# Residual stream kept in token rows, turned by VectorE and DRAM instead of TensorE, with three sequences of the first layer ahead

## The chip, the cores and the metric

The kernel runs on one core of one Trainium2 chip. Its engines work side by side, each through its own list of instructions in order: PE (matrix products), DVE (vector), ACT (scalar functions), POOL (a general engine) and SP, which here issues all transfers. The metric is the device time of one execution in microseconds (us). All arithmetic is fp32.

## The reference

The input x is (8 sequences, 512 tokens, 256 features). With xn = layernorm(x), the output is x + s * silu(g).

- s is one causal attention over xn with rotary positions, one head of 256.
- g is a transformer of two layers over xn, each with eight heads of 64 and a window of 128 tokens:

```
h = shift_token(x)                 # second half of the features comes from the token before
q, k, v = split(h @ wqkv)          # 256 -> 3 * 512
q, k = l2norm, scale, rotary with xpos
x = x + local_attention(q, k, v) @ wo
h = shift_token(x)
h = (h - mean) / sqrt(var + eps) * lg + lb       # over the shifted 256 features
a, g = split(h @ w1 + b1)                        # 256 -> 2 * 682
x = x + (a * gelu(g)) @ w2 + b2
```

Because the shift stands ahead of the layernorm, the mean and variance of a token mix the first 128 features of this token with the last 128 of the token before.

## The kernel before

A sequence has four tiles of 128 tokens. A *slot* is one layer of one sequence, (b, l); there are 16. They run in the order (0,0), (1,0), (0,1), (2,0), (1,1), ... (7,0), (6,1), (7,1). For each slot: `project` makes q, k and v of each tile (matmuls "qkv"), DVE, ACT and POOL rotate and norm them (tiles r, side, sq, ss, rn), `turn_out` transposes blocks of 32x32 on DVE into rt and sends them to DRAM (away) in an order from which `turns_in` loads qT and kT already transposed. `all_scores` multiplies them ("sps"), masks and exponentiates, `p_out` and `p_in` turn the probabilities in the same way through p_away, `all_sums` multiplies with v ("ops"), `all_outs` multiplies with wo ("wop") and adds to the residual stream, and `feed_forward` does the rest ("ff" is w1, "w2p" is w2). Within layer 0, `start` also does the plain layernorm of x and the causal attention (matmuls "qk", "v0p", "sc", "av"); it parks its result s in DRAM. `finish` loads s and x again, applies silu, multiplies, adds and stores.

The residual stream of a sequence lies in xT with features as partitions: two halves of 128 features, each with 512 tokens as columns; the shift by one token is a matter of which columns a matmul reads. So whatever needs tokens as partitions is transposed on PE against an identity: x itself on arrival (xTp), the stream ahead of the second layernorm (hps), the result ahead of silu (yps). PE also turns the causal probabilities (pT0p). Ahead of ff, normed rows xh are turned back through hn and DRAM (`blocks_back`); the last slot works in two halves of 256 tokens and uses PE for this (hT).

What runs when on PE is written out: the string ORDER names, by a letter per job, which job takes its next step. A planner (class Order) goes through it, keeps a time line for every engine with estimated durations (the numbers in `order.on`, `LAND`, `send`), and places the instructions of DVE, ACT, POOL and SP in the order in which these estimates come due; `keep` fixes that order. On the chip each engine follows its list strictly and waits where an input is missing.

Loads of layer 0's weights come after a block of 32 small transfers that clear parts of eight DRAM areas (`clear_p_aways`), and layer 1's come one by one behind the first steps (`late_loads`).

Of the kernel before, what the change touches and what calls it, by code (L numbers as in the profile page):

```python
# [15 lines left out]
P = 128  # L16
# [22 lines left out]
HALF2 = T + 1  # L39
# [5 lines left out]
    "H2JHFHGH4FHFEF2JHFENEH3FHEHFH2EGF3HF2D2H2ECFHCJGJ2ED2CENF2ECEJ2GFDBJFJCDECJFEJGECBEFC2J"  # L45
    "DFDEFJ2FA2BJIEFJFGFC3J2FJED2CEJBJN2GN2A2IECI2NCF2NFIBNFEN2D2CINFE2N2RICICI4ND2NICIFE2BN"
    "F2NRCDCDAFAENF2EBCENCFKNK2CR2ERDFRFBFRDACEAEF2EKCRDCRFRFKR2EFDEBEFKECRF2RDCDCFKCKEK2BD2"
    "FC2A2E2RFEF2EBCDC2DEKR2CKLFBCF2EFRA2DLDCFLKF2RFCE2BEC2LKEDLELDFBF2CERCFECFAD2FAFL2CE2F"
    "L2D2E2BCECLF3BOLCFEDCDAOAC2OELFBCFOEFCF2E2OLBM2D2FCMFOAEAMOF2OMEFCDCDCOEFOEFOPEBVCDFCFO"
    "EFPFBDEFCRFAFDEDVFE2AVC2OFPVBPVCVCVCOD2BEFCVECEPF3VDFDCAPAVFPVFEBC2FPCFEFEFPD2BEVPFCEPE"  # L50
    "F3PFD2VEFSAEC2AEVS2CVFVBEDSECPCPDQBCSFEVFACSFDCDVQF2ASCBQF2QVCEFESQVEFCZVSD2BETFSFCF2E2"
    "ZSFESD2T2CZCACEAZEZSETZ2STFBECDCDETFZFZBDCDFEFCTECFAFAWBCE2CTECZTFDFDBTFTFECATZD2ZCWAF2"
    "WFEWETEWFZCZCEFTD2BEFC2EZUFUZCFZBCEWUFW2CD2ZAUWACBUF3ZEWCXF2CEWFWXBdD2EZF2CFEFEWdZDC2DC"
    "XdFEA2E2dWBCX2EFXCd3BD2CEFEFdCd2F2E2XFdFD2EACXFAXCBEDEDCdFXF2EXCXFd2BCECDEDdF3ACaCEFXAa"
    "dFaD2BC2FXEBaFC2aFEFdCFEAEdAYFdYEdD2CBYFCFYabF2Ea2YCaFaD2CBEChFEdEa2AFbAFh2EbCD2bFEahEb"
    "CahF2EbFBED2hChEFChbEBD2bF2EFCAEC2bFABECDECDFbeCFEbF2BF2bFeCAD2eCEFACE2bFe2hCBCDFDFChb"
    "E3BC2F2DEeCDAF2eFEACeEeBDECDhFcF2E2FCe2hfeBCE2CD2CfFfF2A2CFecBfCEhfEFCeBD2fECcFEF2EhA2E"
    "F2fD2iFC2fEfFcfCD2BC2F2CEfFBfEFCECAEAiFiFiBD2C2FEiFEfFfDEDEC2ghi4Ei3BD2iCicAhF2CFEAFCBC"
    "EFj2CFjEF2BhA2FjDhE2jh2F2DECFgFhCDEjDgCFgFjEjECjEBC2gjED2EjBjFC2A2DCl2DlCj2klBCk2lkl2C"
    "l3BlA2nkn2l2n2m3on7ono2"  # L60
# [19 lines left out]
class Order:  # L80
# [12 lines left out]
        "quarters": {"full": 0.22, "rows": 0.2, "columns": 0.165, "eighths": 0.165},  # L93
        "eighths": {"full": 0.22, "rows": 0.2, "columns": 0.165, "quarters": 0.165},
# [150 lines left out]
def gated_attention_kernel(  # L245
# [27 lines left out]
    counts = {"x": 1, "xT": 4, "r": 7, "rt": 1, "v0": 1, "oT": 1, "hn": 1, "hid": 1, "tok": 2}  # L273
# [66 lines left out]
    def send(dst, src, after, us):  # L340

        sync.dma_start(dst, src)
        return order.on("SP", 0.42, after) + us
# [28 lines left out]
    for l in range(DEPTH):  # L372
        sc = buffer("tok", [P, 4, DH], f"sc{l}")
# [3 lines left out]
        vec_sb = weights.tile([P, 3 * KC + 2 * HC], F32, tag=f"vec{l}", name=f"vec{l}")  # L377
# [8 lines left out]
    def loads_of(l):  # L386
# [8 lines left out]
        def queries():  # L395
            load(f"wqkv{l}", wqkv_sb, wqkv[l].rearrange("(k p) n -> p k n", p=P))
# [10 lines left out]
        def second():  # L407
            load(
                f"w2{l}", w2_sb[:, 0 : HC - 1, :], w2[l, 0:whole].rearrange("(k p) n -> p k n", p=P)
            )  # L410

            for n in range(KC):
                on, cols = n * DH, slice(n * P, (n + 1) * P)
                load(f"w2{l}", w2_sb[on : on + TAIL, HC - 1, cols], w2[l, whole:HID, cols])

        return [attention, queries, output], [lambda: first(0), lambda: first(1), second]
# [14 lines left out]

    before, behind_x = loads_of(0)
# [4 lines left out]
    scale_tables(0)  # L437

# [3 lines left out]
    def layernorm(dst, src, n, name, at=0.0, groups=False):  # L442


        kind = name[0]
        few = 2 if kind == "x" else 4
        stats = small.tile([P, n, 6], F32, tag=f"stats{kind}", name=f"stats_{name}", bufs=few)
        mv = small.tile([P, n, 2], F32, tag=f"mv{kind}", name=f"mv_{name}", bufs=few)
        for i in range(n):
            vector.bn_stats(stats[:, i], src[:, i])  # L450
            end = order.on("DVE", 0.41, at, opens=f"stats{kind}")
        for i in range(n):
            vector.bn_aggr(mv[:, i], stats[:, i])
            at = order.on("DVE", 0.16, end, opens=f"mv{kind}")
        rstd = small.tile([P, n], F32, tag=f"rstd{kind}", name=f"rstd_{name}", bufs=few)
        gpsimd.tensor_scalar(rstd[:, 0:n], mv[:, 0:n, 1], EPS, None, ALU.add)
        at = order.on("POOL", 0.23, at, opens=f"rstd{kind}")
        inv_sqrt(rstd[:, 0:n], rstd[:, 0:n], n)
        at = order.on("POOL", 0.4 + 0.16 * n, at)
        for i in range(n):  # L460
            to, some = dst[:, i], src[:, i]
            if groups:
                to = to.rearrange("p (g c b) -> p c g b", g=4, c=KC)
                some = some.rearrange("p (c g b) -> p c g b", g=4, c=KC)
            vector.tensor_scalar(
                to, some, mv[:, i, 0:1], rstd[:, i : i + 1], ALU.subtract, ALU.mult
            )
            end = order.on("DVE", 0.54 if kind == "h" else 0.41, at, opens="tok" if kind == "h" else "")
        return end

    slots = [(0, 0)]
    for b in range(1, BATCH):
        slots += [(b, 0), (b - 1, 1)]
    slots.append((BATCH - 1, 1))
    stream, gated = {}, {}
# [9 lines left out]
    def start(b):  # L487
        yield {"free": {"x": 1, "xT": 1} if b else {"xT": 1}}
# [3 lines left out]
        xt = x_tiles.pop(b)  # L492
# [3 lines left out]
        xT = buffer("xT", [P, 2 * T + 1], f"xT_{b}")  # L496
        nc.gpsimd.memset(xT[:, T : T + 1], 0.0)
        yield {"at": at, "free": {"bank": 2}}
        for c in range(KC):
            ps = bank(f"xTp_{b}_{c}").rearrange("p (a b) -> p a b", a=NT)  # L500
            for t in range(NT):
                transpose(ps[:, t, :], xt[:, t, c * P : (c + 1) * P])
            at = evacuate(xT[:, c * HALF2 : c * HALF2 + T], ps.rearrange("p a b -> p (a b)"))
            free(f"xTp_{b}_{c}", at)
        free(f"x_{b}")
        stream[b] = xT
        done("started", b, at=at)

# [6 lines left out]
        for n in range(2):  # L515
            even, odd = rot[n]
            for e in range(2):
# [6 lines left out]
                for k in range(KC):  # L524
# [3 lines left out]
                        xT[:, k * HALF2 : k * HALF2 + T],  # L528
# [6 lines left out]
                else:  # L535
                    vector.tensor_mul(ta, ps, sin)
                    vector.tensor_mul(odd, ps, cos)
                at = max(
                    order.on("DVE", 0.69, arrived["rope"], opens=opens)
                    for opens in (("r", "side") if e == 0 else ("sq", "r"))  # L540
                )
# [8 lines left out]
        for t2 in range(NT // 2):  # L550
            yield {"free": {"bank": 1}}
            ps = bank(f"v0p_{b}_{t2}").rearrange("p (a e) -> p a e", a=2)
            for a in range(2):
                t = 2 * t2 + a
                for c in range(KC):
                    matmul(
                        ps[:, a],
                        xT[:, c * HALF2 + t * P : c * HALF2 + (t + 1) * P],
# [6 lines left out]
        done("read", b)  # L565

        s = dram.tile([P, NT, DIM], F32, tag="s", name=f"s_{b}")
        gated[b] = s
# [31 lines left out]
        def turn(t):  # L600
            p, at = ps_p.pop(t)
            yield {"at": at, "free": {"bank": 1, "r": 1}}
            tps = bank(f"pT0p_{b}_{t}").rearrange("p (a b) -> p a b", a=NT)
            for j in range(t + 1):
                transpose(tps[:, j, :], p[:, j * P : (j + 1) * P])
            free(f"p0_{b}_{t}")
            pT = buffer("r", [P, 4, P], f"pT0_{b}_{t}")
            at = evacuate(pT[:, 0 : t + 1], tps[:, 0 : t + 1], "r")
            free(f"pT0p_{b}_{t}", at)
            turned[t] = pT, at + order.HOP  # L610

# [766 lines left out]
```

## Time and profile before

| | us |
|---|---|
| three runs | 1316.09, 1318.51, 1318.78 (median 1318.51) |
| the profiled execution | 1317.86, span 1316.0, mean PE clock 0.993 |
| PE busy | 1288.7 (98%) |
| DVE busy | 1006.5 (76%) |
| ACT busy | 732.8 (56%) |
| POOL busy | 627.5 (48%) |
| transfers | 1236 issued by SP, 214.87 MB, 57.4% of the 16 DMA engines' time |

Reading it: "busy" is the time in which at least one instruction of the engine ran; neighbouring matmuls overlap, so the busy times of groups add up to more than the engine's. "PEld" is the load of the stationary operand, which runs beside the products. A releaser ("<- DVE x") is what ended an engine's wait. "us to landing" of a transfer is from its issue to its completion. In the slices a 9 is 90% or more.

### The profile page before, as it was taken

How to read it: one execution, taken by the hardware profiler on the slowest of the kernel's cores; microseconds unless marked ns; L12 is line 12 of the kernel's file. 1: busy time of each engine (PE TensorE's matmuls, PEld its weight loads, DVE VectorE, ACT ScalarE, POOL GpSimd, SP SyncE). 2: the span in 40 equal slices, each digit the busy share in tenths (PEclk: the TensorE clock that was granted, in tenths of full speed). 3: DMA queues.
4: the chain of work that ended last, by engine and by line, in shares of the span. 5: the costliest groups of instructions: out<-in, count | busy, mean ns of one | idle time of the engine just before them, and what ended most of it. 6: DMA issues, size and time to landing. Idle time of an engine off the chain costs nothing.

```text
span 1316.0 us, 30660 instructions
## 1 busy us (share of the span) xinstructions
PE 1288.7 (98%) x11010; PEld 731.7 (56%) x11010; DVE 1006.5 (76%) x3088; ACT 732.8 (56%) x1955; POOL 627.5 (48%) x651
## 2 busy tenths in 40 slices
PE   9779999999999999999999999999999999999998
PEld 4446555565554565555655555555455555545467
DVE  6667858888778887878788787788878778866864
ACT  2345444774647556564656637556565638553753
POOL 6647516635455646354534455544535454425500
PEclk9889999999999999999999999999999999999999
DMA  5768535665556555664646564567455665544761
GB/s 197 214 207 227 165 97 137 197 182 156 173 164 195 161 151 162 174 184 132 182 115 205 145 179 130 146 198 195 137 164 143 182 175 164 169 117 113 232 169 57
DMA packets 273239, 216.83 MB, mean 165 GB/s; under 512 B 21016, under 2 KB 244416, under 8 KB 273088
## 3 DMA queue, kind: packets, MB, share of 16 engines
q1 hardware_dynamic: 273088, 214.87, 57.4%
q8 instruction: 88, 1.44, 0.5%
q14 instruction: 63, 0.52, 0.1%
HBM read 124.09 MB, written 90.70 MB: 163 GB/s over the span
## 4 chain that ended last, share of the span: by engine, by line
PE 89%; DMA 4%; DVE 2%; SPq 2%; issue 1%; ACT 1%; POOL 0%; DVEq 0%; ACTq 0%
PE ff L304 23%; PE qkv L304 23%; PE w2p L304 12%; PE wop L304 8%; PE ops L304 6%; PE sps L304 6%; PE qk L304 3%; PE sc L304 2%; PE av L304 2%; DMA qT<-away 2%; PE v0p L304 2%; SPq L73 2%; PE hps L308 1%; DMA kT<-away 1%; DMA x<-in_x_dram 1%
## 5 line engine op out<-in xcount | busy, mean ns | idle before, releaser
L73 POOL TENSOR_TENSOR r<-r,side 128x512 f32<-128x512 f32 x128 | 163.0, 1273 | 447.6 <-DVE side L73 402.4
L304 PE MATMUL qkv<-wqkv,xT 128*128 128x512 f32 x768 | 359.5, 599 | 0.2
L304 PE MATMUL ff<-hn,w 128*128 128x512 f32 (+1 forms) x680 | 284.9, 568 | 0.0
L73 ACT ACTIVATE p<-p,nmx 128x160 f32<-128x160 f32 (+1 forms) x512 | 209.1, 410 | 73.5 <-DVE nmx L73 72.7
L304 PEld LDWEIGHTS qkv<-wqkv,xT 128*128 128x128 f32 x768 | 141.1, 191 | 141.2 <-issue 128.2
L73 POOL TENSOR_TENSOR rn<-ss,neg_half 128x8 f32<-128x8 f32 x128 | 214.3, 1674 | 10.7
L304 PEld LDWEIGHTS ff<-hn,w 128*128 128x128 f32 x680 | 128.1, 190 | 135.7 <-issue 122.2
L304 PE MATMUL w2p<-hid,w 128*128 128x512 f32 (+3 forms) x408 | 159.5, 576 | 0.0
L73 DVE CUSTOM_DVE_ANT_0 p<-sps,mask_sb 128x160 f32<-128x160 f32 (+1 forms) x512 | 132.1, 307 | 14.8 <-PE sps L304 14.6
L73 POOL TENSOR_TENSOR r<-r,rn 128x512 f32<-128x512 f32 x128 | 133.8, 1045 | 10.0
L73 ACT ACTIVATE p<-p,rden 128x160 f32<-128x160 f32 (+1 forms) x287 | 114.1, 413 | 41.2 <-DVE rden L73 39.5
L73 ACT ACTIVATE sq<-qkv 128x512 f32<-128x512 f32 x128 | 75.1, 592 | 95.8 <-PE qkv L304 86.3
L73 DVE STREAM_TRANSPOSE pr<-p 128x320 f32<-128x320 f32 (+1 forms) x256 | 116.1, 477 | 15.1 <-ACT p L73 10.6
L73 DVE SCALAR_TENSOR_TENSOR hid<-ff,vec,hid 128x512 f32<-128x512 f32 (+3 forms) x119 | 83.8, 713 | 54.3 <-PE ff L304 26.8
L73 ACT ACT_TABLE_LOAD x96 | 123.2, 1283 | 2.4 <-PEq L1368 0.7
L304 PE MATMUL wop<-oT,wo 128*128 128x256 f32 x512 | 118.9, 381 | 0.3 <-DVE oT L73 0.3
L73 DVE TENSOR_TENSOR r<-qkv,tables 128x512 f32<-128x512 f32 x128 | 86.8, 678 | 37.8 <-ACT sq L73 33.6
L304 PEld LDWEIGHTS w2p<-hid,w 128*128 128x128 f32 (+1 forms) x408 | 68.8, 189 | 80.1 <-issue 78.3
L73 DVE STREAM_TRANSPOSE rt<-r 128x512 f32<-128x512 f32 x128 | 90.1, 704 | 29.9 <-POOL r L73 23.4
L304 PEld LDWEIGHTS wop<-oT,wo 128*128 128x128 f32 x512 | 96.2, 190 | 27.5 <-issue 12.6
L304 PEld LDWEIGHTS ops<-pT,v 64*64 64x64 f32 x3584 | 83.2, 134 | 37.0 <-issue 27.2
L73 ACT ACTIVATE hid<-ff,vec 128x512 f32<-128x512 f32 (+2 forms) x102 | 66.4, 662 | 66.3 <-PE ff L304 65.5
(82 smaller groups left out, 1681.6 us busy)
## 6 DMA issues: line engine op xcount, KB each, us to landing
pT<-p_away SPq DMA_DIRECT2D x96, 384.0 KB, 4.5
away<-rt SPq DMA_DIRECT2D x256, 128.0 KB, 2.6
kT<-away SPq DMA_DIRECT2D x112, 256.0 KB, 3.7
p_away<-pr SPq DMA_DIRECT2D x160, 128.0 KB, 2.4
qT<-away SPq DMA_DIRECT2D x64, 256.0 KB, 3.8
p_away<-pr SPq DMA_DIRECT2D x96, 96.0 KB, 1.9
pT<-p_away SPq DMA_DIRECT2D x32, 256.0 KB, 3.4
hn_away<-hn SPq DMA_DIRECT2D x60, 128.0 KB, 2.5
```

The source lines that it names most:

```text
L73: ins = getattr(self.engine, name)(*args, **kwargs)
L304: nc.tensor.matmul(out, lhsT=lhsT, rhs=rhs, start=start, stop=stop)
L308: nc.tensor.transpose(out, in_, ident)
```

## The change

- The residual stream stays in x_tiles, tokens as partitions, four buffers. wop and w2p now produce token rows (the activations are the stationary operand and the weights move), and are added there. b2 is an extra row of w2, multiplied with a row of ones in hid_sb.
- Matmul inputs with features as partitions are made anew where needed: `turn_stream` transposes 32x32 blocks on DVE, sends four pieces to DRAM and loads four pieces (runs of 32 elements) back as xT. This is done for x of sequences 2 to 7 and for every sequence between the layers. Sequences 0 and 1 still use PE for x.
- The causal p of sequences 1 to 7 is turned the same way (tiles p0_away).
- The second layernorm takes its statistics from halves of 128 features in token rows. For the shifted half, those of the token before are fetched from the partition before: `neighbours` issues four transfers within the tile "sides". The normed rows are turned through DRAM into hn, with the shift as an offset of one column; the first token's missing neighbour is done by `first_row`.
- silu and the output work on x_tiles in place; the yps transposes go.
- Slots run (0,0), (1,0), (2,0), (0,1), (3,0), (1,1), (4,0), ... (5,1), (6,1), (7,1).
- wqkv is loaded in four pieces, wo and what follows later; each area p_away is cleared ahead of its first use. ORDER is new throughout.

```
-HALF2 = T + 1
+FIRST = T + 1
+AHEAD = 3
...
-    counts = {"x": 1, "xT": 4, "r": 7, "rt": 1, "v0": 1, "oT": 1, "hn": 1, "hid": 1, "tok": 2}
+    counts = {"x": 4, "xT": 2, "r": 7, "rt": 1, "v0": 1, "oT": 1, "hn": 1, "hid": 1}
...
+        def queries(k, to=3 * INNER):
+            some = slice(to - 3 * INNER // 2, to)
+            load(f"wqkv{l}", wqkv_sb[:, k, some], wqkv[l, k * P : (k + 1) * P, some])
...
+    slots = [(b, 0) for b in range(AHEAD)]
+    for b in range(BATCH):
+        slots += [(b, 1)] if b + AHEAD >= BATCH else [(b, 1), (b + AHEAD, 0)]
...
+    def turned_out(staged, away, at):
+        rows = away.rearrange("(g b) (s n) -> s b g n", g=4, s=4)
+        for s in range(4):
+            mine = staged[s * BLOCK : (s + 1) * BLOCK].rearrange("b (g n) -> b g n", g=4)
+            there = send(rows[s], mine, at, LAND[128])
+        return there
+
+    def turned_in(staged, away, at):
+        to = staged.rearrange("p (n s a) -> p s n a", s=4, a=BLOCK)
+        src = away.rearrange("p (s n a) -> p s n a", s=4, a=BLOCK)
+        for s in range(4):
+            there = send(to[:, s], src[:, s], at, LAND[128])
+        return there
+
+    def turn_stream(b, l, at):
+        xT = buffer("xT", [P, 2 * T + 1], f"xT_{b}_{l}")
...
+        for t in range(0, NT, 2):
+            for c in range(KC):
+                vector.transpose(
+                    blocks[:, :, 1 - c, t : t + 2].rearrange("p g t a -> p t g a"),
+                    x_tiles[b][:, t : t + 2, c * P : (c + 1) * P].rearrange("p t (g b) -> p t g b", g=4),
+                )
...
+            there = turned_out(staged, away, at)
+        landed = turned_in(staged, away, there)
...
         def turn(t):
+            if b == 0:
...
+            vector.transpose(
+                staged.rearrange("p (k a) -> p k a", a=BLOCK), p[:, 0:n].rearrange("p (k b) -> p k b", b=BLOCK)
+            )
...
+            for s in range(4):
+                mine = staged[s * BLOCK : (s + 1) * BLOCK].rearrange("b (k a) -> b k a", a=BLOCK)
+                there = send(rows[s], mine, at, LAND[128])
...
+            landed = send(pT[:, 0 : t + 1], away.rearrange("(j p) q -> p j q", p=P), there, LAND[256])
...
-                    for c in range(IC):
-                        w = wo_sb[:, c, m * P : (m + 1) * P]
-                        matmul(ps, w, oT[:, c], c == 0, c == IC - 1)
+                for a in range(2):
+                    for c in range(IC):
+                        matmul(ps[:, a], oT[:, c, a * P : (a + 1) * P], wo_sb[:, c], c == 0, c == IC - 1)
+                two = x_tiles[b][:, 2 * half : 2 * half + 2]
+                vector.tensor_add(two, ps, two)
...
+        def neighbours(tiles, at):
+            lo, hi = tiles[0], tiles[-1] + 1
+            moves = [
+                (side[1:P, lo:hi, 0], side[0 : P - 1, lo:hi, 2]),
+                (side[0 : P - 1, lo:hi, 3], side[1:P, lo:hi, 1]),
+            ]
+            lo = max(lo, 1)
+            moves += [
+                (side[0:1, lo:hi, 0], side[P - 1 : P, lo - 1 : hi - 1, 2]),
+                (side[P - 1 : P, lo - 1 : hi - 1, 3], side[0:1, lo:hi, 1]),
+            ]
+            for dst, src in moves:
+                there = send(dst, src, at, 2.3)
+            return there
...
-            hps = bank(f"hps_{b}_{l}_{t2}").rearrange("p (a f) -> p a f", a=2)
-                    transpose(
-                        hps[:, a, c * P : (c + 1) * P],
-                        xT[:, c * T + t * P : c * T + (t + 1) * P],
-                    )
...
+            for h in range(KC):
+                vector.bn_stats(side[:, t, 1 + h], xt[:, t, h * P : (h + 1) * P])
+        there = neighbours(mine, at)
+        normed = normal(sets, there)
...
-                w = w2_sb[:, c, m * P : (m + 1) * P]
-                matmul(ps[m], w, hid[:, c, part], starts, stops)
+                        lhsT = hid_sb[:, c, t * P : (t + 1) * P]
+                        matmul(place(t), lhsT, w2_sb[:, c], c == 0 and t % 2 == 0, False)
...
-                yps = bank(f"yps_{nm}")[:, 0 : 2 * n].rearrange("p (a f) -> p a f", a=2)
-                scalar.activation(g, yps, AF.Silu)
+            y = x_tiles[b][:, some]
+            scalar.activation(y, y, AF.Silu)
```

## The prediction

> **What bounds the kernel now.** I read the page first (engine totals, slices), then the table of time stretches, the waits of PE alone, the chain that ended last between 1200 and 1316 us, and the DMA issues.
>
> ```profile
> span 1316.0 us, 30660 instructions
> ...
> PE 1288.7 (98%) x11010; PEld 731.7 (56%) x11010; DVE 1006.5 (76%) x3088; ACT 732.8 (56%) x1955; POOL 627.5 (48%) x651
> ```
> ```profile
> 0.00:100.00 100.00, 82.15 (x562) 45.72 (x562) 63.90 (x197) 38.03 (x114) 57.88 (x72) 0.91 0.68 205
> ...
> 200.00:1200.00 1000.00, 997.99 (x8785) 555.99 (x8784) 794.74 (x2442) 580.18 (x1546) 490.30 (x498) 1.00 0.58 163
> ...
> 1280.00:1316.00 36.00, 31.30 (x209) 25.64 (x207) 14.24 (x31) 11.57 (x19) 1.72 (x2) 0.98 0.20 63
> ```
> ```profile
> PE pT0p L308 <- ACT p L73: 6.5, 1, 6.5
> PE sps L304 <- DMA p_away<-pr: 6.5, 1, 6.5
> ```
> In the columns (stretch, length, busy us of PE, weight load, DVE, ACT, POOL) PE is busy for 998 of the middle 1000 us at clock 1.00. Its idle time is 18 us in the first 100 and 5 at the end. So in the middle a change pays by taking work off PE, and costs as soon as it makes PE wait; PE executes a list written out by hand and overtakes nothing.
>
> What one PE instruction is worth on this path I take from the chain, where pieces don't overlap:
>
> ```profile
> 1201.06 0.44 PE hps L308 x4
> 1201.50 3.44 PE qkv L304 x8
> ...
> 1208.34 3.47 PE wop L304 x16
> ...
> 1246.33 1.33 PE sps L304 x64
> ...
> 1261.13 0.61 PE hps L308 x4
> ```
> A transpose is 0.11 us, a 512-column matmul instruction 0.43 (fp32 takes two per product), a 256-column one 0.217. The same four transposes take 0.61 after a switch of array shape (sps to full), so a switch is 0.17.
>
> **PE, part by part.** Gone: 128 hps, 64 yps, 48 of 64 xTp and 70 of 80 pT0p transposes; hT grows from 8 to 9. 309 x 0.11 = -34.0 us. wop and w2p exchange weights and moving operand. wop is as wide as before. w2p becomes twice as many 256-column products; wop shows two of them cost one of 512 (0.217 against 0.43), weight loads included: 0. The new order switches shape 253 times outside w2's last rows, where the old one did 234 times: +19 x 0.17 = +3.2. Net **-31 us**, bounds -28 to -34.
>
> **Start.** Of the 18 us idle, 13 are the two waits above; in that time SP issued 32 clearings of p_away (20 us of its queue). These move to the first eight steps with a second block, four each; wqkv comes in four pieces, the second and third x before w2, and two more sequences offer PE work. But 8.2 MB of loads still come first, some 24 us at the 350 GB/s of the busy stretches. Between 0 and -16; I take **-10**. **End:** yps goes, while add, silu, two DVE passes and store remain: 0 (-1 to +1).
>
> **Other engines.** DVE: 56 stream-transposes of 128x256 (0.44) +25, 28 for causal p (0.32 to 0.70) +14, half-width bn_stats +10, aggr +10, half-width normalising +8, edges +4; less copies, wo adds and p scalings -18: +53 us, 1059 in all, covered by its 310 idle us only while those are not used up by waits. ACT loses about 10, POOL changes by under 2. SP issues 1644 transfers instead of 1236: 408 x 0.42 = 171 us more. DVE and SP run in order as well.
>
> **The new chain before ff.** Before: hps, statistics, normalise, turn, out, in, gain. Now the statistics of the shifted half come from the neighbouring token's partition: bn_stats on halves, four transfers inside "sides" (two of 127x4x6, two of 1x3x6), then bn_aggr. For a whole slot, in us: add 0.7, four bn_stats 1.1, sides S, eight aggr 1.3, POOL 0.25 + 1.7 (its 128x8 power), eight half-width subtractions 2.4, two stream-transposes 1.4, four sends out 3 x 0.44 + 2.5 = 3.8, four in 3.9, first gain 0.8: 17.4 + S. S is the unknown. Spread over 16 engines, four issues and a landing like the smallest row here give 1.9 + 1.8 = 3.7; need 21.1, about 22 with hops.
>
> What covers it is the PE list between the second wop and the first ff. Timing it with the prices above, I get for the 15 whole slots 17.6, 23.0, 23.1, 23.7, 27.0, 27.1, 27.9, 30.3, 30.4, 31.0, 32.9, 45, 52, 58 and 128 us. (For 23.7: 2 ff, 8 qkv, 64 sps, 16 ops, 24 w2p and 4 av instructions, sps and ops counted singly.) In 27.0, 27.9, 30.4 and 32.9, DVE's list holds 4 to 8 us of other work inside the chain, so they are no looser than 23. Nine slots have 1 to 2 us to spare, one some 3, two some 6, three plenty. The old kernel's shortest such gap (16.3) equals its chain, and PE never waited at ff, so a plan this tight does work if the times hold.
>
> ```profile
> hn<-hn_away SPq DMA_DIRECT2D x15, 512.0 KB, 4.4
> ...
> p_away<-pr SPq DMA_DIRECT2D x96, 32.0 KB, 1.8
> ...
> w<-in_w_dram SPq DMA_DIRECT2D x4, 21.0 KB
> vec<-in_vecs_dram SPq DMA_DIRECT2D x2, 9.0 KB, 5.3
> ```
> **What S is.** The 21 KB row is 42 partitions. In the trace's completion records such a transfer gives one completion at issue and 14 later, where transfers of 128 or 32 partitions give 16: 42 rows went to 14 engines in equal shares of three. No row has unequal shares. Equal shares of 127 rows exist only on one engine. A 127x4x6 transfer is 508 pieces of 24 bytes; the nearest row is vec, whose 72-byte packets follow each other by 8 ns and take 12. On one engine that is 4.1 to 6.1 us per transfer, two of them one behind the other: S = 0.5 + 8.1 + 1.8 = 10.4 (to 14.5). If shares need not be equal (eight rows on most engines), S = 3.7. I take 10.4, since every row seen has equal shares, and keep both ends.
>
> The Trainium skill ("DMA: Bandwidth & Descriptors", section "Why a DMA increments its semaphore by 16 and not by 1") states that the engine count is the largest number up to 16 that divides the slowest dimension, and names 127 partitions as one engine. By it the case would be as taken here, and the sum 1346; against it 1277.
>
> At S = 10.4 a tight slot is 6.7 - 1.5 = 5.2 us late: 9 x 5.2 + 3.7 + 2 x 0.7 = 52 us. Behind the late bn_aggr DVE stops (its list has only about 4.3 us of other work there), with the masks of sps and the emptying of PSUM banks queued on it; and every transfer issued in those 8 us has a share behind the 1016 pieces on that engine, with SP stopping at the eighth transfer after, as completions are shared by eight in turn. Attention's chains have 16 to 20 us of PE list where they need 15 to 16, so some are late in the slots where ff is not: between 0 and 5 us per slot; I take 1.1 x 15 = 17. Stalls **+69**, bounds +20 and +110.
>
> **128-byte pieces.** Turning in (hn, xT) and causal p now move 128-byte pieces, 4096 for a whole tile. The nearest row, 168-byte packets, take 15 ns: 256 per engine are 3.8 us, the time in which four issues pass anyway: +0, up to +2 per slot. The same page ("Specifications") says that under 512 bytes the line rate is lost; the trace agrees (168 bytes in 15 ns, 512 in 27), and at that loss it would still be 3.8 us. From w2's end to the next layer's qkv the list holds 14 to 160 us for about 10.5; causal scores to av at least 10.7 for 10.0: no stall.
>
> **Sum.** The profiled execution took 1317.9 us (span 1316.0 and 1.9 around it; the median of the three runs is 1318.5): 1317.9 - 31 - 10 + 0 + 69 = 1346.
>
> **Rivals.**
> - *The neighbours' transfers are spread (S = 3.7).* Then nothing waits and PE's shorter list decides: 1317.9 - 31 - 10 = 1277, 1262 to 1300 with a few short waits. For it: the old plan was as tight and held. Against: equal shares. It decides where S stays under about 6 us; with stalls of 41 us in all the two kernels are even.
> - *DVE and the queues become the bound.* 1059 us of DVE work and 15 stops of 6 us are 1150 of some 1300, and DVE was idle for 205 of the middle 1000 us on other waits already. If all of those persist, attention is late in every slot too: 110 us of stalls and more, 1386 to 1430. Against: DVE's waits are mostly for PE and shrink when PE is late.
> - *The list is shorter but time is unchanged*, stalls of 39 to 44 us: 1316 to 1321. Only by coincidence.
>
> **Chances.** One engine and stalls as summed: 0.55, 1321 to 1385. Spread or hidden, faster: 0.29. DVE and queues: 0.12. Same: 0.04. Likeliest 1346. The range reaches into the spread case and into the third: 1274 to 1405, leaving out 0.2. A measurement of this kernel tells 0.2% (2.6 us) from no change. Faster 0.29, same 0.04, slower 0.67.
>
> **What would show it.** No hps and yps on PE, w2p in 256 columns with unchanged time per column. Right: sides landing 6 to 11 us after issue, DVE waiting at mv_h some 6 us in most slots, PE waiting at ff on hn by about 50 us in all, PE busy near 1255. Wrong: sides landing near 2 us and PE without waits in the middle; or large PE waits elsewhere (sps or ops on transfers, av on p). The start is right if the first 100 us hold 5 to 10 us of PE idle time.

## The result and the profile after

The changed kernel takes 1450.33 us (median of four runs, 1449.51 to 1451.24), beside 1317.63 for the kernel before on the same chip: a ratio of 1.1008 [1.0989, 1.1027]. It is slower, as forecast, but by 133 us where 28 were forecast: 1346 was predicted, and 1405 was the upper end of the range. (Medians of the kernel before in the series of runs below lie between 1317 and 1319; so 2 us between two series aren't told from noise.)

The page of the changed kernel: its span, the busy times, the clock granted to PE in 40 slices, and the shares of the chain that ended last.

```profile
span 1449.0 us, 31654 instructions
...
PE 1306.5 (90%) x11061; PEld 783.1 (54%) x11061; DVE 1044.4 (72%) x3328; ACT 732.7 (51%) x1950; POOL 625.9 (43%) x629
...
PEclk9899899999789999999999989999899899999999
...
PE 47%; DMA 16%; SPq 14%; DVE 12%; ACT 4%; POOL 3%; issue 3%; DVEq 0%; POOLq 0%; ACTq 0%
```

PE has a list with less work, and yet was busy 17.8 us longer (1306.5 against 1288.7), while it stood idle for 142.5 us instead of 27.3. The two make up the 133 us by which the span grew. The chain no longer runs through PE: it is PE for 47% of the span, and for 30% transfers and SP's own issuing.

The table of time stretches of the changed kernel (stretch, length, busy us of PE, weight load, DVE, ACT, POOL, then the granted clock):

```profile
0.00:100.00 100.00, 83.15 (x556) 45.42 (x557) 74.73 (x237) 41.06 (x125) 64.19 (x78) 0.91 0.76 224
100.00:200.00 100.00, 87.99 (x814) 52.54 (x814) 74.65 (x251) 52.34 (x154) 49.30 (x48) 0.91 0.71 179
200.00:1200.00 1000.00, 907.21 (x7800) 538.11 (x7799) 730.59 (x2324) 507.02 (x1353) 436.82 (x430) 0.95 0.66 163
```

In the middle 1000 us, where PE was idle for 2 before, it is idle for 93, and its clock is 0.95 instead of 1.00. The first 200 us hold 29 us of idle time instead of 18. DVE is less busy per 1000 us than before (731 against 795): it isn't the bound.

What PE waited for in the changed kernel (total us, times, longest), and what DVE waited for longest:

```profile
PE ops L313 <- DMA pT<-p_away: 31.8, 10, 10.0
PE sps L313 <- DMA qT<-away: 24.4, 13, 5.0
PE ff L313 <- ACT hn L82: 23.8, 8, 6.6
PE qkv L313 <- DMA xT<-x_away: 11.9, 4, 6.3
PE ops L313 <- DVE rden L82: 11.0, 2, 8.9
```
```profile
DVE mv_h L82 <- DMA sides<-sides: 75.6, 29, 4.1
```

The forecast put the stalls at ff. They are there, at 24 us, but 56 us are attention's: its transposed probabilities (pT) and its q (qT) come late, though the change leaves the way they are made as it was. The column is the last releaser only; what stands before these transfers is in the chain and in the list of transfers. Around one neighbour exchange, the chain that ended last (start, length, piece) and SP's own timeline:

```profile
747.74 0.78 DVE sides L82 x4
749.37 3.33 SPq L82
752.75 3.07 SPq L82
755.86 1.66 DMA sides<-sides
```
```profile
748.54 7.98 SPq L82 DMA_DIRECT2D sides<-sides  x4
756.69 0.36 SPq L82 DMA_DIRECT2D p<-p_away  x1
757.11 0.42 SPq L82 DMA_DIRECT2D pT<-p_away  x1
```

From 748.54 to the landing at 757.52 is S = 9.0 us, near the 10.4 of the prediction. What the prediction didn't have is that SP itself is held for 8 of them. The first transfer of 127 partitions is issued in 0.78 us; the issue behind it, which is the second of them, takes 3.33 us, and the issue behind that one, of a single partition, 3.07. It is so in all 15 whole exchanges (0.75 to 0.83, then 3.04 to 3.59, then 2.75 to 3.08, then 0.65 to 0.67 us). A load of pT waits behind them in SP's list until 757. A neighbour exchange thus delays whatever SP was to send next, which here is attention's.

How PE's longest wait came about shows the same order of things: the exchange, then the load that PE waits for.

```profile
374.20 7.68 SPq L82 DMA_DIRECT2D sides<-sides  x4
390.44 0.47 SPq L82 DMA_DIRECT2D pT<-p_away  x1
393.84 1.12 PE L313 MATMUL ops<-pT,v 64*64 64x128 f32 x16 [10.03 <-DMA pT<-p_away]
```

Between the two, SP issued other transfers that had come due meanwhile, so not all of the 10 us is the exchange's.

The issues by tile, before and after (least, median and most ns that one issue took on SP; before first):

```profile
L73 SPq DMA_DIRECT2D hn<-hn_away x15: 319/337/1859, 145.2 to 1221.2; - x15
```
```profile
L82 SPq DMA_DIRECT2D hn<-hn_away x60: 370/730/2457, 161.0 to 1363.2; - x60
L82 SPq DMA_DIRECT2D xT<-x_away x56: 371/666/1878, 88.4 to 1294.3; - x56
L82 SPq DMA_DIRECT2D sides<-sides x68: 592/1222/3592, 131.4 to 1418.6; - x68
```

An issue isn't 0.42 us whatever it moves. Loads in runs of 128 bytes take twice as long to issue, and four of them stand where one was. The durations of all of SP's issues sum to 938 us in the changed kernel and to 586 before: 352 us more, where the prediction had 171.

Last, the clock. Time stretches of 2 us of the changed kernel around a wait of 2.40 us for xT that ends at 706.92:

```profile
704.00:706.00 2.00, 0.52 (x3) 0.12 (x1) 1.40 (x2) 1.97 (x3) 0.00 (x0) 1.00 1.08 144
706.00:708.00 2.00, 1.07 (x3) 0.63 (x4) 0.00 (x0) 1.41 (x5) 0.00 (x0) 1.00 0.69 200
708.00:710.00 2.00, 2.00 (x5) 0.73 (x4) 0.66 (x2) 0.00 (x0) 0.00 (x0) 0.58 0.00 0
710.00:712.00 2.00, 2.00 (x4) 0.86 (x3) 1.93 (x6) 1.62 (x5) 0.88 (x1) 0.57 0.00 0
712.00:714.00 2.00, 2.00 (x9) 1.47 (x8) 2.00 (x5) 1.10 (x3) 0.43 (x2) 1.00 0.01 4
```

PE is at work again from 706.9 on, but from 708 to 712 its clock is little over a half in the mean: the clock's record is 0.50 from 708.3 on for 3.41 us, and 1.00 around it. The eight qkv products behind this wait took 5.37 us in the chain, where eight elsewhere take 3.43:

```profile
308.32 3.43 PE qkv L313 x8
706.92 5.37 PE qkv L313 x8
```

So a wait can be paid for twice, once while PE stands and once after. Counted in stretches of 1 us, the changed kernel's clock falls below 0.9 in 20 places, that of the kernel before in two, both in the first 100 us, and as it ends. The Trainium skill ("TensorE: Matmul & The Clock Gate", section "What's actually happening") gives half the rate when idle, judged in windows of about 3.4 us; the depth and length of this stretch agree. The wait of 2.40 us is shorter than such a window, though, so what counts as idle here can't be a whole window without work.

The records of the clock are 1.00 or 0.50 throughout. So PE's work can be stated apart from the clock: its busy time, less half of what lies in stretches at 0.50. That is 1283.2 us before and 1258.8 in the changed kernel. The 133 us by which the span grew are then 24 us less work, 42 us more for the lowered clock (47.7 against 5.5) and 115 us more of standing idle.

### The profile page after: what moved, and what is told of

Read it like the earlier page. It is cut to its first block, busy times and chain, and to the rows that moved or that the text cites. A ratio compares the mean times of both kernels' runs of the same rounds, so it can differ in the third digit from the quotient of the medians.

```text
span 1449.0 us, 31654 instructions
## 1 busy us (share of the span) xinstructions
PE 1306.5 (90%) x11061; PEld 783.1 (54%) x11061; DVE 1044.4 (72%) x3328; ACT 732.7 (51%) x1950; POOL 625.9 (43%) x629
## 4 chain that ended last, share of the span: by engine, by line
PE 47%; DMA 16%; SPq 14%; DVE 12%; ACT 4%; POOL 3%; issue 3%; DVEq 0%; POOLq 0%; ACTq 0%
SPq L82 14%; PE qkv L313 13%; PE ff L313 13%; PE wop L313 6%; PE ops L313 4%; PE w2p L313 3%; PE sps L313 3%; PE qk L313 2%; DMA p_away<-pr 2%; DMA away<-rt 2%; DMA pT<-p_away 2%; ACT p L82 2%; DMA hn<-hn_away 2%; DMA qT<-away 2%; DVE x L82 2%
## 5 line engine op out<-in xcount | busy, mean ns | idle before, releaser
L313 PE MATMUL qkv<-wqkv,xT 128*128 128x512 f32 x768 | 377.8, 626 | 17.1 <-DMA xT<-x_away 11.9
L313 PE MATMUL ff<-hn,w 128*128 128x512 f32 (+1 forms) x680 | 292.8, 582 | 26.1 <-ACT hn L82 23.8
L313 PE MATMUL w2p<-w,hid_sb 128*128 128x256 f32 (+1 forms) x768 | 160.7, 384 | 2.7 <-DVE nmx L82 2.7
L313 PE MATMUL ops<-pT,v 64*64 64x128 f32 (+1 forms) x3584 | 105.6, 263 | 49.8 <-DMA pT<-p_away 31.8
L313 PEld LDWEIGHTS w2p<-w,hid_sb 128*128 128x128 f32 (+1 forms) x768 | 131.8, 189 | 32.9 <-issue 13.9
L82 DVE STREAM_TRANSPOSE pr<-p 128x320 f32<-128x320 f32 (+4 forms) x284 | 129.4, 477 | 24.0 <-ACT p L82 12.5
L313 PEld LDWEIGHTS ops<-pT,v 64*64 64x64 f32 x3584 | 92.4, 144 | 87.4 <-issue 48.8
L313 PE MATMUL sps<-kT,qT 64*32 64x160 f32 (+1 forms) x4096 | 92.2, 306 | 32.7 <-DMA qT<-away 24.4
L313 PE MATMUL wop<-wo,oT 128*128 128x256 f32 x512 | 116.4, 380 | 0.0
L313 PEld LDWEIGHTS wop<-wo,oT 128*128 128x128 f32 x512 | 96.6, 190 | 24.6 <-issue 10.6
```

What stands on the lines that cost most here:

```text
L82: ins = getattr(self.engine, name)(*args, **kwargs)
L313: nc.tensor.matmul(out, lhsT=lhsT, rhs=rhs, start=start, stop=stop)
```

## The experiments

**Is it the one-engine transfers?** *split* cuts each transfer of 127 partitions at 112, so that the larger part divides by 16.

```
-            moves = [
-                (side[1:P, lo:hi, 0], side[0 : P - 1, lo:hi, 2]),
-                (side[0 : P - 1, lo:hi, 3], side[1:P, lo:hi, 1]),
-            ]
+            moves = []
+            for on, to in ((0, 112), (112, P - 1)):
+                moves += [
+                    (side[on + 1 : to + 1, lo:hi, 0], side[on:to, lo:hi, 2]),
+                    (side[on:to, lo:hi, 3], side[on + 1 : to + 1, lo:hi, 1]),
+                ]
```

> The changed kernel with each 127-row transfer of the neighbours' statistics cut into one of 112 rows and one of 15 (six transfers in place of four; the same result). Theory A (the two 127-row transfers hold up SP's queue and one DMA engine for 8 us per slot, and that is behind most of PE's waits): SP's time on them falls from 131 us to under 50, DVE's waits ahead of bn_aggr from 76 to under 25, PE's idle time from 142 to 50 to 80, the mean clock rises from 0.95 to 0.98, and the time falls to about 1340 (1310 to 1375). Theory B (the many new transfers and 128-byte pieces are behind it, sides is only where it is seen): the time stays above 1410.

1415.25 us, 1.0727 [1.0693, 1.0760]: 35 us less than the changed kernel, by far not the 1340 of theory A. What the cut was to do, it did: an exchange holds SP for 4.8 us instead of 7.7, and DVE's wait at mv_h falls from 75.6 to 27.9 us. That it was one engine is in the completion records, too: after its issue, a transfer of 127 partitions has one completion (at 753.59 and 756.70 in the exchange above), one of 112 partitions in split has 16.

```profile
DVE mv_h L82 <- DMA sides<-sides: 27.9, 19, 4.2
```

*nofetch* makes no neighbour transfers at all; it fills their places in sides once, at the start.

```
-        for t, place in ((0, 0), (NT - 1, 3)):
+        for t, place in [(t, place) for t in range(NT) for place in (0, 3)]:
...
-            for dst, src in moves:
-                there = send(dst, src, at, 2.3)
-            return there
+            return at + 4.0
```

> The changed kernel without the four transfers of the neighbours' statistics: bn_aggr reads places in sides that were filled once at the start, so the variances and means of the second layernorm are not those of the reference; all else is done. It bounds what the whole step can be worth. Theory A: 1300 to 1340, and not more than 25 us below the split version. Theory B: above 1400.

1386.85 us, 1.0508 [1.0464, 1.0551], between the two theories. So the neighbour exchange costs 63.5 us in all: 35 go with the cut at 112, and the 28 that are left go with the six transfers. What PE waits for in split and in nofetch:

```profile
PE ops L313 <- DMA pT<-p_away: 28.0, 13, 8.7
PE ff L313 <- ACT hn L82: 27.1, 9, 6.8
PE sps L313 <- DMA qT<-away: 23.8, 10, 6.4
```
```profile
PE sps L313 <- DMA qT<-away: 24.6, 12, 6.1
PE ops L313 <- DMA pT<-p_away: 15.9, 5, 4.8
PE ff L313 <- ACT hn L82: 13.4, 6, 4.2
PE pT0p L317 <- ACT p L82: 12.7, 1, 12.7
```

In split these three are together what they were (79 us against 80): what the cut took away were PE's other waits (62 us before it, 38 after), those for DVE's rden and sides among them, and 8 us of the clock. In nofetch the waits at ff and for pT are halved, that for qT remains. The exchange is about half of the loss; the other half (1387 against 1318) has another source.

Two things limit these prices. The first: nofetch, and the three runs below that are built on it, have a wait of 12.7 us for the first pT0p, where the changed kernel waits for 2.5. They do 12 more bn_stats at the start, and the planner then orders DVE's start another way; PE is idle for 24 us of the first 100 instead of 17. The exchange is thus priced some 7 us too low, and what remains in these runs too high, if that delay carries through to the end (an estimate from these idle times). The second: each edit gives the planner other times, and it reorders DVE, ACT and SP, while PE's list stays the same. Of the changed kernel's 3328 DVE instructions some 3070 keep their order in split and some 2910 in nofetch. A difference between two runs is the edit with its new order; *told*, below, shows what an order alone can do.

**What does a wait of PE cost?** *twice* adds two more round trips of hn through DRAM to the kernel before, ahead of ff in 15 slots.

```
+            for _ in range(2):
+                landed = send(away, hn.rearrange("p c n -> p (c n)"), landed, LAND[512])
+                landed = send(hn.rearrange("p c n -> p (c n)"), away, landed, LAND[512])
```

> The kernel before with two more round trips of hn to DRAM and back ahead of ff in 15 slots (same result), some 20 us longer a chain, of which the plan's slack covers a part. PE should wait at ff for 60 to 140 us more in all. Theory C (a wait of PE of more than some 2 us lets its clock drop, which costs about 2 us more afterwards): the busy time of PE rises too, by 20 to 40 us, and the clock falls to 0.97 to 0.98. Rival (a wait costs its length only; the changed kernel's lower clock has another cause): busy time unchanged within 5 us.

1597.51 us, 1.2108 [1.2072, 1.2145]. The wait at ff in this run:

```profile
PE ff L304 <- ACT hn L73: 238.5, 15, 20.7
```

PE waits longer than expected, and its busy time grew by 36.1 us (1324.8 against 1288.7) with the same instructions. Of these, 32 lie in stretches at clock 0.50 (37.7 us lost to them, against 5.5 before): 2.1 us for each of the 15 waits, on top of the wait. That is the clock's share, measured on the old list.

**What do the changed kernel's extra issues and DVE work cost by themselves, on the old list?** *pieces* loads hn back in four transfers of 128-byte runs.

```
-            landed = send(hn.rearrange("p c n -> p (c n)"), away, there, LAND[512])
...
+            for s in range(4):
+                landed = send(to[:, s], src[:, s], there, LAND[128])
...
```

> The kernel before with hn loaded back in four transfers of 128-byte runs, as the changed kernel does it, and ff reading contiguous columns (same result). Theory B: issuing and landing of such pieces is dear, PE waits for 30 us and more, time 1345 or above. Theory A: SP spends some 45 us more, the chain is 4 us longer, most of it covered: 1318 to 1335.

1327.88 us, 1.0067 [1.0043, 1.0091], as theory A had it. *spload* adds 384 tiny transfers on SP.

```
+        idle_issues(3)
```

> The kernel before with 384 more transfers on SP (three after each turning-out of q and k, three after each turning-out of p; 4 KB each, into DRAM that nobody reads; same result), some 170 to 190 us of issuing, as much as the changed kernel's 408 more transfers. Theory B2 (what remains in the split and nofetch versions is SP's queue: more issues, each in its turn, so that the transfers PE waits for leave late): PE waits 30 to 90 us more, mostly for qT and pT, and the time is 1350 to 1410. Rival (issuing alone is covered; something else is behind the rest): under 1330.

1336.33 us, 1.0136 [1.0116, 1.0155], between the theory and its rival, with qT's wait at 8.5 us instead of 3.2. *dveload* adds 128 stream-transposes of 128x256 on DVE, of which nothing is used.

```
+        vector.transpose(
+            spare.rearrange("p (g c b) -> p c g b", c=2, g=4),
+            mask_sb[:, 0 : 2 * P].rearrange("p (c g a) -> p c g a", c=2, g=4),
+        )
```

> The kernel before with 128 more stream-transposes of 128x256 on DVE, into a tile that nobody reads, one after each transpose of q and k (same result): 56 us more of DVE work, what the change adds. Theory E (DVE in its fixed order, now busier, makes attention's chains late): PE waits 20 to 60 us more, 1340 to 1375. Rival (covered): below 1328.

1358.82 us, 1.0340 [1.0296, 1.0384]: 40 us and more for 56 us of work (a net 31 on DVE's total, as the planner moved some scalings of p to ACT) on an engine that was idle for 310. The added work also gave DVE another order (some 2430 of its 3088 instructions keep theirs), so the 40 us are not the load's alone. *three* does all three.

> The kernel before with the 384 more issues on SP, hn in 128-byte pieces and the 56 us more on DVE together (same result). If their costs only add up: 1318 + 19 + 9 + that of dveload alone. Theory G (each takes slack from the same chains, so together they cost more than the sum): 15 us or more above that sum, and the clock below 0.98.

1380.92 us, 1.0503 [1.0467, 1.0539]. The parts' sum, unrounded, is 5.4%, and 5.0% was measured: they add up, and don't amplify each other.

**Is it the turning that should go back to PE?** *splitpe* is split with the stream and the causal p transposed on PE again, at the places that PE's list has for them.

```
-        there = turned_out(staged, away, at)
-        yield {"at": there - 1.0}
-        landed = turned_in(staged, away, there)
...
+        for c in range(KC):
...
+            for t in range(NT):
+                transpose(ps[:, t, :], x_tiles[b][:, t, c * P : (c + 1) * P])
...
```

> The split version with the stream and the causal p turned by PE again (182 more transposes on PE, 20 us; 252 transfers fewer on SP), token rows and the list of PE's order kept; same result. Theory B2: PE's idle time falls from 117 to 30 to 60 us and the clock rises to 0.98; the time is 1340 to 1370, below split's 1415 by 45 to 75. Rival (the order itself or the chain of the second layernorm): 1400 or above.

1499.90 us, 1.1384 [1.1362, 1.1407]. Waits that the changed kernel had at 0.4 and 2.5 us:

```profile
PE xTp L317 <- DVE x L82: 50.4, 6, 21.7
PE pT0p L317 <- ACT p L82: 41.6, 16, 6.2
```

The run doesn't answer the question: the list has these steps where DVE and DRAM could start them, and PE, which takes them in order, stands there until the input exists. To undo this part one would have to move it in the order as well.

**Is it the planner's wrong prices?** *told* is split, with the planner given the issue and landing times that the changed kernel showed; the order of DVE, ACT, POOL and SP then changes, PE's doesn't.

```
-            there = send(to[:, s], src[:, s], at, LAND[128])
+            there = send(to[:, s], src[:, s], at, 3.5, issue=0.85)
```

> The split version, its planner told the measured durations of transfers (0.52 us an issue in place of 0.42, 0.85 and 3.5 us for a 128-byte piece of a turn in place of 0.42 and 2.6, 0.81 for the neighbours' transfers), so that DVE, ACT, POOL and SP have their instructions in another order; PE's list and all work unchanged. Theory D (the fixed order on DVE and SP, planned with times that don't hold, makes engines stop at late inputs): 1415 falls to 1395 or below. Rival: within 10 us of split.

1469.54 us, 1.1149 [1.1131, 1.1167], 54 us slower than split, where 20 us less, or at most 10 either way, was expected: prices nearer to the measured ones, with the same PE list, make it worse. The prices alone are not the cause. It also says what an order is worth: PE's list and the work are those of split, some 2740 of DVE's 3330 instructions keep their order, and that makes 54 us.

**The rest, transfer by transfer.** *nopieces* is nofetch with hn and xT loaded back in one transfer of 4 KB rows, as hn was before. The columns then stand in another order, and what is computed from them isn't the reference's.

```
...
-        for s in range(4):
-            there = send(to[:, s], src[:, s], at, LAND[128])
-        return there
+        return send(staged, away, at, 3 * 0.42 + LAND[128])
```

> The nofetch version with each tile (hn, xT) loaded back in one transfer of 4 KB rows in place of four of 128-byte pieces, so that the columns are in a wrong order as well; all else is done. Theory F (the 128-byte turns, planned with 3.9 us and taking about 6.9, make ff and the next layer's qkv late): 1350 to 1372, from 1387. Rival (they are covered): 1380 or above.

1350.97 us, 1.0264 [1.0234, 1.0294]: 36 us less. Here nearly the whole order stays (some 3290 of DVE's 3354 instructions), so this is the loads' price, as far as the new order lets it be told; whether by their 87 further issues or by the short runs isn't separated. *nocausal* also drops the transfers of the causal p.

```
-            for s in range(4):
-                mine = staged[s * BLOCK : (s + 1) * BLOCK].rearrange("b (k a) -> b k a", a=BLOCK)
-                there = send(rows[s], mine, at, LAND[128])
+            there = at + 3.0
...
```

> The nopieces version without the transfers of the causal p (140 fewer on SP; av multiplies the p that was not turned, so s is wrong). Theory B2 in its weaker form (every transfer in SP's queue takes a little slack from attention): 8 to 20 us below nopieces. Rival: within 5 us of it, and what is left lies in the order of PE's list and its start.

1335.10 us, 1.0137 [1.0111, 1.0163]: 16 us less, again with nearly the same order. What shrinks is not a wait for the causal p but attention's: that for pT goes from 19.4 to 8.5 us, that for qT from 19.7 to 16.7. *noturn* also drops DVE's transposes of the stream and sends it out in one transfer.

```
...
-        there = turned_out(staged, away, at)
+        there = send(away, x_tiles[b].rearrange("p t f -> p (t f)"), at, 3 * 0.42 + LAND[128], "xT")
```

> nocausal, and the stream isn't turned either: the 56 stream-transposes of 128x256 on DVE are gone and the four sends of a tile out are one (x is loaded back unturned, so that the result isn't the reference's). Question: what the 48 us are that the last kernel (1335) still lies above 1287 (the time before less 31 us of PE work). Theory H, DVE: 56 transposes with about 0.5 us each are 28 us off DVE and 42 issues off SP; by the run in which 56 us more on DVE cost 42 us, the time falls by 15 to 25, to 1310 to 1320, and PE's waits in the middle shrink. Theory I, the order and the start: DVE has room, the time stays at 1330 to 1336.

1331.96 us, 1.0107 [1.0089, 1.0125]. Only 3 us, and the two intervals overlap: here DVE's 56 transposes (0.44 us each, 25 in all; DVE's total falls by 17) were covered, unlike the added ones on the old list. What is left, in noturn's page and PE's waits:

```profile
PE 1271.7 (95%) x11061; PEld 766.1 (57%) x11061; DVE 1028.3 (77%) x3300; ACT 730.6 (55%) x1934; POOL 627.3 (47%) x629
```
```profile
PE sps L313 <- DMA qT<-away: 14.3, 5, 7.0
PE pT0p L317 <- ACT p L82: 12.8, 1, 12.8
PE ops L313 <- DMA pT<-p_away: 10.5, 6, 5.9
PE ff L313 <- ACT hn L82: 4.9, 4, 2.0
```

With nearly all that the change added taken away, PE still waits for 61 us instead of 27, 12 us of the growth in the first 200 us and 22 in the middle (975.69 busy of 1000), with the largest part for attention's own qT and pT: 25 us, where the old list let 4 through. The 12.8 us for pT0p are the delay at the start that these runs have of their own. The rest is what the new order, PE's and the planner's, leaves; why it covers attention's transfers less wasn't found.

**The start.** *clear* is the kernel before with the areas p_away cleared at first use.

```
-        clear_p_aways()
...
+            clear(away)
```

> The kernel before with one part of the change alone: each area p_away is cleared ahead of its first use (32 transfers moved out of the start, same result). Predicted step: the start gains from it; the idle time of PE in the first 100 us falls from 18 to 6 to 12 and the time by 5 to 13 us, to 1306 to 1313. Rival: the weights' loads bound the start, or the clearings delay the first probabilities: 1316 or above.

1315.22 us, 0.9973 [0.9959, 0.9986] over ten runs: the idle time of the first 100 us falls from 18 to 15, where 6 to 12 were expected. It is 2 to 5 us faster than the kernel before, the lowest median of all these runs. *late* has this too, and adds the changed kernel's later loads of w1 and w2 and layer 1's loads in pairs.

```
-        for some in behind_x:
-            some()
+        for n, key in zip(range(3), steps[1:]):
+            yield {"after": [event("parked", *key)]}
+            behind_x[n]()
...
```

> The kernel before with the areas cleared at first use, and with what follows layer 0's wqkv and wo (w1, w2) loaded in three pieces behind the first three steps instead of at once, layer 1's in pairs behind the next ones: the load order of the changed kernel on the old list. If the loads ahead of the second x hold the start up, the 15 us of idle time in the first 100 us fall to 8 or less and the time to 1306 to 1312, and the start's 10 us of the prediction are to be had with the old order. If the start is held by the chains and not by the loads, it stays at 1313 to 1317.

1316.27 us, 0.9988 [0.9978, 0.9999], with 14 us idle in the first 100: no better than clear. On the old list the start isn't held by these loads; by the rival of this experiment, it is held by its chains.

## Why the prediction was right on the sign and wrong on the size

The steps that failed are three. Transfers and the issuing of them were priced at nothing where they stood beside the path (the 128-byte pieces, the causal p): 36 and 16 us. The clock had no term: 42 us. And the stalls were priced as if the new order left attention's other transfers the cover that the old one gave them: 41 us that remain when the new transfers are gone, the start with them, which was to gain 10 and gained nothing.

Read from the bottom up, the runs give the changed kernel's time as a sum: 1291 (the time before less the 27 us of work that PE has less in noturn), 41 for the new order and its start (noturn), 3 for turning the stream on DVE and sending it in four, 16 for the causal p's transfers, 36 for the 128-byte loads, 28 for the neighbour exchange cut at 112, 35 for its running on one engine: 1450. Each difference includes the clock that its waits cost, and the planner's new order; some 7 of the 41 belong to the exchange if the delay at the start of these runs is taken out. So 16 and 36 stand firmest, 28 and 35 less.

- **PE's work, -31: right in kind, 4 to 7 us too large.** With the clock taken out as above, the work is 1283.2 us before, 1258.8 in the changed kernel and 1256.2 in noturn, which has the same PE list: 24 to 27 us less, where the bounds were 28 and 34. The eight kernels here with the old PE list lie between 1282 and 1288 by this measure, the seven with the new one between 1256 and 1259. w2p, at twice the products of half the width, is busy 160.7 us against 159.5: the 0 was right.
- **S = 10.4 and 69 us of stalls: the mechanism was right, its place was not.** S is 9.0, on one engine as predicted; DVE waits at mv_h as foreseen, if 2.6 us on average (75.6 over 29) and not 6. That the exchange costs 63.5 us, near the 69, is luck, as the parts show: ff got 24 us of waits instead of 52, and attention 56 instead of 17. The Trainium skill's rule on the engine count ("DMA: Bandwidth & Descriptors", section "Why a DMA increments its semaphore by 16 and not by 1") held for 127 partitions, and split, at 112 and 15, bears it out. But the step "SP stopping at the eighth transfer after" was the wrong reading of what SP does: SP is held in the next two issues, at 3.33 and 3.07 us, and loads that stand behind them are attention's. That this hold is what made attention late is shown for single waits only: in split, where it is 3 us shorter, attention's waits are still 52 us. The count of tight slots doesn't come out of the gaps that the prediction lists, either: a gap of 17.6 us is shorter than the 21.1 needed even at S = 3.7.
- **128-byte pieces, +0: the step that failed by 36 us.** It took the issue at 0.42 us ("the time in which four issues pass anyway"), reckoned 3.9 us for four pieces in, and set the price between 0 and 2 us a slot; 36 us are a little over 2. In the changed kernel the median issue is 0.73 and 0.67 us, and where landings are listed (nofetch) a piece takes 4.3 us for hn and 3.9 for xT in the median, the first three issues coming on top. The causal p's "at least 10.7 for 10.0: no stall" nearly held for av itself (one wait of 3.7 us for p); what was missing is what these 140 issues cost elsewhere, 16 us in nocausal: as attention's waits are what shrinks there, most likely by standing ahead of its transfers in SP's list. The 171 us of added issuing, from 408 x 0.42, were 352.
- **No term for the clock.** The waits were priced at their length. Those that were long enough cost some 2 us more each; the 20 places of lowered clock took 47.7 us of PE's busy time, 42 more than before. These are nearly a third of the loss. The row was in the profile of before: there, four qkv products behind the 6.45 us wait that ends at 47.6 took 3.56 us instead of 1.9.
- **Start, -10: wrong.** The first 100 us hold 17 us of idle time, not 5 to 10, and the first 200 hold 29, 11 more than before. That the loads are not what holds the start up is shown by late, for the old list.
- **DVE's +53 us at 0: neither shown right nor wrong in the changed kernel.** DVE's busy time grew by 38. In noturn 17 of them go, for 3 us; on the old list 56 us cost some 40, with DVE's order changed. What "covered by its 310 idle us" left out is that idle time is only cover where it lies in the right places; that the old list, with 1 or 2 us to spare in its tight slots, has little there fits dveload, but is argued.
- **The rivals.** "DVE and the queues become the bound" came nearest, with 1386 to 1430: attention's waits are the largest, 56 us in 23 of them. But DVE is not the bound (busy for 731 of the middle 1000 us); nocausal and the held issues speak for SP's queue, spload, at 19 us for 384 issues, says that issuing alone isn't enough. The spread case (1277) fell: split, which spreads them, is at 1415.

What stays open: the 41 us of the new order. PE's list and the planner's order come together, and the one run that gave the new kernel another order of the planner's (told) was worse. How much of 28 and 35 is the order's is open for the same reason.

## What to carry to other kernels

A transfer's price has a part on the issuing queue: here it doubled with runs of 128 bytes, and where the partition count left a transfer on one engine it came to 3 us on the issue behind. Price it from an issue row of the same shape, and look at what stands behind it in that queue. Where PE is the bound and its profile shows a lowered clock behind waits, add what that costs: here some 2 us for each wait that was long enough. Before moving work to an engine with idle time, ask where in the slot that idle time lies: 310 idle us didn't hide 56 us of work. And where a planner places the rest, a run that leaves a part out also changes the order, which alone was worth 54 us once: see how much of the order two runs share before taking their difference for the part's price.

## What the runs showed of the hardware that I had not expected

- The issue behind a transfer of 127 partitions by four runs of 24 bytes holds SP for 2.75 to 3.59 us (for 1.6 us where it is two runs), while that transfer's own issue, with nothing like it ahead, takes 0.8. Cut into 112 and 15, the six issues of an exchange take 4.8 us in all.
- A wait of 2.40 us was enough to bring PE's clock to 0.50 for 3.41 us, beginning 1.4 us after PE had resumed; others of 2.89 and 3.30 us were not. The changed kernel's 20 stretches last 3.41 us or two, three or four times that.
- DVE's 25 us of transposes cost some 3 us under the new order, and 56 us of the same transposes some 40 under the old, reordering included.
